# A first half-transfer on ACT's queue, weights loaded later, and convergence products placed in pairs between the last additions

## The chip, the cores and the metric

The kernel runs on one core of one Trainium2 chip. The metric is the device time of one execution in microseconds, taken as the median of three runs. Less is better. A profile was taken of one further execution. Its own time and the span between its first and last instruction stand in the table below.

## The reference, cut to what matters

The input `x` has four images of 128 channels and 64 x 64 = 4096 positions (tokens), all in float32. Three stages follow each other:

```python
# layer 0: attention over channels of a convolution, no causal mask
q, k, v = wq @ x, wk @ x, wv @ x            # 64 x 4096 per image
att = softmax(k.T @ q, over j)              # 4096 x 4096
x   = x + wo @ (att @ v.T).T

# layer 1, attention: on layer-normalised tokens t (4096 x 128)
t = t + softmax(causal(q @ k.T / sqrt(128))) @ v

# layer 1, recurrence: batch-normalised wx_t, 4096 steps per image
y_t = sigmoid(wx_t + y_{t-1} @ V.T)
out = t + y                                  # in the layout of x
```

## The kernel before

The program has two parts. `fast_path` computes everything under two assumptions that it tests on the way: that the softmax denominators stay in a safe range, and that the recurrence forgets its start. The result of the tests is one integer, `flag`. After `fast_path`, every engine loads `flag` (L1277) and branches (L1278); `general_path`, a slow version for the other case, is skipped with these inputs.

**Attention.** The work is a list of items, each a pair of 128-key tiles against one block of 512 queries. `scores` (L894 in layer 0, L903 in layer 1) makes the products on TensorE, ACT takes the exponential (L908, L910), DVE adds up the denominators (L932, L934), and `values` (L954, L962) multiplies by the values two items later. This part lasts from about 14 us to 1975 us.

**The start of image 0.** Layer 0 needs the keys and queries in both halves of the partitions. `cols0` makes the product of 512 columns with `[wq|wk]` (`wqk`, h = 0) and with `[wk|wq]` (`wkq`, h = 1), copies each out of PSUM into `kr` (DVE for h = 0 at L539, ACT for h = 1 at L537), and a DMA (L541) copies 64 partitions of `kr` to the other 64 partitions of `swap`. `vals0` (L547) and `vals0_by_tokens` (L572) make the values. The first scores need the h = 0 half of the first `swap`. The order in the source is: `cols0`, `vals0` of block 0, `cols0` of block 1, `vals0_by_tokens` of block 0, then the items. The list `side` holds the other blocks; one of its tasks goes between two items.

**Queues.** SP's queue issues the eight transfers of `x` of image 0 (L426, 256 KB each) and, behind them, the `swap` transfers. ACT's queue issues the three first weights (`wqk`, `wkq`, `wv0`, L414) in five transfers. POOL's queue issues the weights that come later: `wo2`, `wqT`, `wkT`, `wv1` (L414), and `wf`, `vf`, `gamma`, `beta` (L513). Twelve products of `ident` with itself (L496) run on TensorE before the first real product.

**The recurrence and the end.** Time is cut in 256 chunks of 16 steps per image. All chunks run at once, first ten warm-up steps and then 16 real ones, four images in turn: product (L1156, PE), addition (L1158, DVE), sigmoid (L1161, ACT). For images 0 and 1 POOL adds the residual (L1168) and SP stores (L1170). For images 2 and 3, `residual` transposes the states back (L1184, PE, four at a time into one of four PSUM buffers), DVE adds them to `xr` (L1186, 16 additions in all), and SP stores from `xr` (L1191, 12 stores, 4 MB in all). The test of the recurrence compares each image's state after the last step with its start: two products per image into PSUM (L1203 with `ident`, L1204 with `minus`), and on ACT a sum of squares (L1206). `judge` counts (L1212, L1213, DVE), sums over partitions (L1215, PE), and DVE writes `flag` (L1220). `in_range(True)`, called in `third` of the last block, tests the last four denominators in four DVE instructions (L704 to L707).

The order of the instructions on each engine is decided by a scheduler when the program is built; `keep_in_program_order` binds an instruction to the order of the source.

Of the kernel before, what the change touches and what calls it, by code (L numbers as in the profile page):

```python
# [9 lines left out]
F32 = mybir.dt.float32  # L10
AF = mybir.ActivationFunctionType
ALU = mybir.AluOpType
# [3 lines left out]
P = 128  # L16
BLK = 512
# [3 lines left out]
STEPS = 16  # L21
BY_C = 2
# [337 lines left out]
def fast_path(  # L360
# [22 lines left out]
    nc = tc.nc  # L383
    B, C, N = x.shape
    M = c_wqT.shape[1]
    assert C == P and M == P // 2 and N % CHUNK == 0
    NT = N // P
# [66 lines left out]
    wfc = const.tile([P, P], F32, name="wfc")  # L454
    gamma = const.tile([P, 1], F32, name="gamma")
    beta = const.tile([P, 1], F32, name="beta")
    wo2 = load(nc.gpsimd, "wo2", [P, P], (top, c_woT), (bottom, c_woT))
    wqT = load(nc.gpsimd, "wqT", [P, P], (whole, a_wqT))
    wkT = load(nc.gpsimd, "wkT", [P, P], (whole, a_wkT))
    wv1 = load(nc.gpsimd, "wv1", [P, P], (whole, a_wv))  # L460
    good = const.tile([P, 2], F32, name="good")
    g1 = const.tile([P, P], F32, name="g1")
    recs = const.tile([P, 2, B, NT], F32, name="recs")
# [18 lines left out]
    with tc.tile_pool(name="batch", bufs=1) as batch, tc.tile_pool(name="rows", bufs=2) as rowp, tc.tile_pool(  # L482
# [9 lines left out]


        wp = misc("warm_ps")
        for _ in range(12):
            nc.tensor.matmul(wp[:, :P], lhsT=ident, rhs=ident, start=True, stop=True)  # L496

        def form_half():
# [7 lines left out]
        def form():  # L506
            gp = misc("g_ps")
            nc.tensor.matmul(gp[:, :P], lhsT=wqT, rhs=wkT, start=True, stop=True)
            nc.vector.tensor_copy(g1, gp[:, :P])

        def load_rest():
            for t, src in ((wf, f_wT), (vf, f_vT), (gamma, f_gamma), (beta, f_beta)):
                nc.gpsimd.dma_start(out=t, in_=src)  # L513

        class Batch:
            pass
# [7 lines left out]
        def cols0(b, m):  # L524

            bt = bs[b]
            if m == 0:
                bt.kr = batch.tile([P, 2, N // 2], F32, tag="kr", name="kr")  # L530
                bt.swap = batch.tile([P, N // 2], F32, tag="swap", name="swap")
                bt.v = batch.tile([P, NT // 2, 2, M], F32, tag="v", name="v0")
            for h, w in enumerate((wqk, wkq)):
                ps = misc("kr_ps")
                nc.tensor.matmul(ps, lhsT=w, rhs=xs[:, b, ts(m + h * NB // 2, BLK)], start=True, stop=True)
                if h:
                    nc.scalar.copy(bt.kr[:, h, ts(m, BLK)], ps)  # L537
                else:
                    nc.vector.tensor_copy(bt.kr[:, h, ts(m, BLK)], ps)  # L539
                rows, keys = slice(M - h * M, P - h * M), slice(h * M, h * M + M)  # L540
                nc.sync.dma_start(out=bt.swap[keys, ts(m, BLK)], in_=bt.kr[rows, h, ts(m, BLK)])  # L541

        def vals0(b, m):

# [154 lines left out]
        def in_range(last):  # L699

            r = recs.rearrange("p l b t -> p (l b t)")
            r = r[:, -TPB:] if last else r[:, :-TPB]
            r2 = wk.tile([P, BLK], F32, tag="den", name="r2")[:, : r.shape[-1]]
            nc.vector.tensor_scalar(r2, r, LOW, None, ALU.is_ge)  # L704
            nc.vector.tensor_scalar(r, r, HIGH, None, ALU.is_le)
            nc.vector.tensor_tensor(r, r, r2, ALU.mult)
            nc.vector.tensor_reduce(good[:, 1:2] if last else good[:, 0:1], r, AX.X, ALU.add)  # L707
# [50 lines left out]
        def finish1(b, g):  # L758
# [12 lines left out]
            def first():  # L771
                if final:

                    nc.scalar.activation(spare, agg[:, 0:1], AF.Sigmoid)
                denominators(1, b, g, mem["own"])
                joined(1, b, g, projected(1, agg))
                if final:
                    warm(9, agg[:, : BLK // 2])
                if b >= BY_C:
                    nc.sync.dma_start(  # L780
                        out=x2t[b - BY_C, ts(g, BLK)].rearrange("(j p) c -> p j c", p=P),
                        in_=xs[:, b, ts(g, BLK)].rearrange("p (j c) -> p j c", c=P),
                    )
                mem["xh"] = wk.tile([P, TPB, P], F32, tag="xh2", name="xh2")
                mem["of"] = moments(b, g)

            def norm():
                normed(b, g, mem["xh"], *mem["of"], final)
# [32 lines left out]
            def third():  # L821

                to = xs[:, b, ts(g, BLK)].rearrange("p (s c) -> p s c", s=STEPS)
                if final:
                    in_range(True)
                    for k in range(2):
                        wp = misc("wx_ps")[:, : BLK // 2]
                        nc.tensor.matmul(wp, lhsT=wfc, rhs=mem["xhT"][:, ts(k, BLK // 2)], start=True, stop=True)
                        nc.vector.bn_stats(ends[:, 3 + 6 * k : 9 + 6 * k], wp)
                        nc.scalar.copy(to[:, :, ts(k, CPB // 2)], wp.rearrange("p (c s) -> p s c", s=STEPS))  # L830
                    warm(6, mem["xhT"][:, : BLK // 2])
                    return
                wp = misc("wx_ps")
                nc.tensor.matmul(wp, lhsT=wf, rhs=mem["xhT"], start=True, stop=True)
                nc.vector.bn_stats(stats[:, b * NB + g], wp)  # L835
                if b == B - 1 and g == NB - 2:
                    ahead()
                    in_range(False)
                nc.scalar.copy(  # L839
                    to.rearrange("p s (j q u) -> p s j q u", q=Q, j=TPB),  # L840
                    wp.rearrange("p (q j u s) -> p s j q u", q=Q, j=TPB, s=STEPS),
                )
# [208 lines left out]
        for s in range(len(items) + SKEW + 16):  # L1051
            begin(s)
            if SKEW < s < len(items) - 1 and items[s - SKEW].first and items[s + 1].layer == 0:
                ended = items[s - SKEW - 1]
                if ended.layer == 0 and ended.g not in visits[0]:
                    begin(s + 1)
            if 0 <= s - SKEW < len(items):
                it = items[s - SKEW]
                values(it)
                if it.last:  # L1060
                    rows()
                    tokens()
                    for k, g in enumerate(visits[it.layer].get(it.g, ())):
                        push(s, bs[it.b].leave[g](8 * k))
                    push(s, (finish1 if it.layer else finish0)(it.b, it.g))
            if s < len(items):
                sums(items[s])
            due = [w for w in waiting if w[0] <= s]
            if due:
                w = min(due, key=lambda w: w[0])  # L1070
                waiting.remove(w)
                w[1]()
                push(s, w[2])
            elif side:
                side.pop(0)()
                if not side and items[s].b == 0 and items[s].layer == 0:
                    tokens()
                    load_rest()
                    form_half()
        assert not waiting and not side  # L1080

# [5 lines left out]
    with tc.tile_pool(name="xr", bufs=1) as xrp, tc.tile_pool(name="y", bufs=2) as yp, tc.tile_pool(  # L1087
# [87 lines left out]
            if s >= 0:  # L1175
                add(s)

        def residual(b, pairs=True, then=None):

            for h in range(HALVES):  # L1180
                for s0 in range(0, STEPS, TPB):
                    ps = ps_r.tile([P, TPB, P], F32, tag="r", name="yT_ps")
                    for j in range(TPB):
                        nc.tensor.transpose(ps[:, j], states(b, s0 + j)[:, h], ident)  # L1184
                    t = xr[:, b - BY_C, h, ds(s0, TPB)]
                    tc.keep_in_program_order(nc.vector.tensor_tensor(t, t, ps, ALU.add))  # L1186
                    if pairs and h == 0 and not s0 % (2 * TPB):
                        continue
                    part = slice(s0 - TPB, s0 + TPB) if pairs and h == 0 else slice(s0, s0 + TPB)
                    tc.keep_in_program_order(  # L1190
                        nc.sync.dma_start(out=by_chunk(out_t)[b - BY_C, h, :, part], in_=xr[:, b - BY_C, h, part])  # L1191
                    )
                if then and h == 0:
                    then()

        for b in range(BY_C, B - 1):
            residual(b)


        gap = xrp.tile([P, B], F32, name="gap")  # L1200
        for b in range(B):
            ps = ps_y.tile([P, NCH], F32, tag=f"y{b}", name="gap_ps")
            nc.tensor.matmul((grid if b < BY_C else pair)(ps), lhsT=ident, rhs=prev[b], start=True, stop=False)  # L1203
            nc.tensor.matmul(ps, lhsT=minus, rhs=start[:, b, 1:], start=False, stop=True)  # L1204
            sq = yp.tile([P, NCH], F32, tag=f"y{b}", name="sq")
            nc.scalar.activation(sq, ps, AF.Square, accum_out=gap[:, b : b + 1])  # L1206
        count = xrp.tile([P, B + 2], F32, name="count")
        nc.vector.tensor_copy(count[:, B:], good)

# [5 lines left out]
            nc.tensor.matmul(tp, lhsT=total, rhs=ones, start=True, stop=True)  # L1215
            return tp

        got = []
        residual(B - 1, then=lambda: got.append(judge()))
        nc.vector.tensor_scalar(flag, got[0], P * (B + 2 * B * NT) - 0.5, None, ALU.is_lt)  # L1220


# [62 lines left out]
```

## Time and profile before

| what | value |
|---|---|
| median of three runs | 2053.53 us (2053.29 to 2053.88) |
| the profiled execution's own time | 2054.28 us |
| its span, first to last instruction | 2052.6 us |
| granted TensorE clock, mean | 0.999 |
| PE busy | 2036.8 us (99%) |
| DVE busy | 1486.6 us (72%) |
| ACT busy | 989.1 us (48%) |
| POOL busy | 137.5 us (7%) |
| DMA, mean over the span | 43 GB/s |

The page gives the busy time of each engine, then the span in 40 slices, the DMA queues, the chain of work that ended last and the costliest groups of instructions. A matmul in float32 appears as two records; PE is the matmul, PEld its weight load. In lines of the timeline the columns are: start in us from the span's start, duration or stretch in us, engine, line of the kernel, operation, destination and sources, count, and in brackets the idle time before and what ended it. A letter q behind an engine's name (SPq, ACTq) means its sequencer, which issues DMAs. The time from a DMA's issue to its landing is given beside the issue. Line numbers are those of the kernel before.

### The profile page before, as it was taken

Reading aid. Unit: us, or ns where it says so; the run is one execution under the profiler, and the core shown is the slowest. Engines: PE = TensorE matmul, PEld = TensorE weight load, DVE = VectorE, ACT = ScalarE, POOL = GpSimd, SP = SyncE. Lnnn points to the kernel's source line nnn. Section 1 sums busy time; section 2 is a strip of 40 time slices with the busy share of each in tenths; the row PEclk is TensorE's granted clock in tenths of the full one; section 3 lists DMA queues with packets and bytes.
Section 4 is the critical chain, followed back from the end, with each engine's and each line's share of the span. In section 5 each row is a group of like instructions: output and inputs, shape, how many; then the busy total and the mean of one; then the engine's idle time right before and its main releaser. Section 6 shows DMA issues by size and latency. Waiting matters only on the chain. (4 is left out here: it accounts for less than half of the span.)

```text
span 2052.6 us, 30794 instructions
## 1 busy us (share of the span) xinstructions
PE 2036.8 (99%) x11646; PEld 907.4 (44%) x11646; DVE 1486.6 (72%) x2862; ACT 989.1 (48%) x1071; POOL 137.5 (7%) x237
## 2 busy tenths in 40 slices
PE   9999999999999999999999999999999999999998
PEld 3643354444333345444433335444433334544456
DVE  4799877555889987555588997654578998765568
ACT  4666632323666653333466663333356665333346
POOL 1000011000000011000000001100000000100004
PEclk9999999999999999999999999999999999999999
DMA  3111021231201112222111001123000110210056
GB/s 88 53 33 27 12 42 37 51 79 37 58 2 23 22 22 42 47 62 67 22 53 22 17 17 42 37 68 82 16 17 2 22 23 12 52 42 21 21 115 225
DMA packets 237869, 89.03 MB, mean 43 GB/s; under 512 B 174752, under 2 KB 219296, under 8 KB 237200
## 3 DMA queue, kind: packets, MB, share of 16 engines
q1 hardware_dynamic: 236704, 86.42, 17.7%
q8 instruction: 93, 1.52, 0.3%
q14 instruction: 64, 0.52, 0.1%
q0 software_dynamic: 288, 0.39, 0.1%
q10 hardware_dynamic: 720, 0.16, 0.0%
HBM read 45.84 MB, written 36.89 MB: 40 GB/s over the span
## 5 line engine op out<-in xcount | busy, mean ns | idle before, releaser
L934 DVE TENSOR_TENSOR dsum<-dsum,p 128x1024 f32<-128x1024 f32 x676 | 826.1, 1222 | 429.6 <-ACT p L910 308.5
L908 ACT ACTIVATE p<-s_ps,nshift 128x1024 f32<-128x1024 f32 x512 | 569.3, 1116 | 318.4 <-PE s_ps L894 310.3
L910 ACT ACTIVATE p<-s_ps 128x1024 f32<-128x1024 f32 (+2 forms) x288 | 274.2, 952 | 609.5 <-PE s_ps L903 607.1
L954 PE MATMUL acc<-p,v 64*64 64x512 f32 x4096 | 543.0, 590 | 0.0
L894 PE MATMUL s_ps<-swap,kr 64*64 64x512 f32 x2048 | 539.0, 591 | 2.1 <-DMA swap<-kr 1.2
L894 PE MATMUL s_ps<-kr 64*64 64x512 f32 x2048 | 525.0, 591 | 0.0
L903 PE MATMUL s_ps<-rows,xhT 128*128 128x512 f32 (+3 forms) x1152 | 502.9, 559 | 0.0
L962 PE MATMUL acc<-p,xh 128*128 128x512 f32 (+3 forms) x1152 | 500.9, 557 | 0.0
L962 PEld LDWEIGHTS acc<-p,xh 128*128 128x128 f32 x1152 | 216.2, 190 | 244.3 <-issue 234.2
L903 PEld LDWEIGHTS s_ps<-rows,xhT 128*128 128x128 f32 x1152 | 214.0, 190 | 243.3 <-issue 203.4
L954 PEld LDWEIGHTS acc<-p,v 64*64 64x64 f32 x4096 | 166.6, 133 | 272.5 <-issue 251.6
L894 PEld LDWEIGHTS s_ps<-swap,kr 64*64 64x64 f32 x2048 | 151.4, 133 | 132.3 <-issue 107.7
L894 PEld LDWEIGHTS s_ps<-kr 64*64 64x64 f32 x2048 | 140.7, 133 | 138.0 <-issue 133.6
L666 POOL TENSOR_TENSOR ln_rstd<-ln_var,mhalf 128x4 f32<-128x4 f32 x64 | 68.2, 1065 | 1099.4 <-DVE ln_var L664 1099.4
L942 DVE TENSOR_TENSOR dsum<-dsum,p 128x256 f32<-128x256 f32 (+1 forms) x120 | 55.4, 497 | 64.3 <-POOL p L914 64.3
L652 DVE SCALAR_TENSOR_TENSOR xs<-o_ps,recs,xs 128x128 f32<-128x128 f32 x256 | 74.4, 341 | 3.1
L682 DVE TENSOR_SCALAR xh<-xs,ln_mv,ln_rstd 128x128 f32<-128x128 f32 x252 | 70.2, 342 | 2.2
L914 POOL TENSOR_SCALAR_AFFINE_SELECT p<-p 128x128 f32<-128x128 f32 x128 | 35.9, 304 | 486.4 <-ACT p L910 473.9
L661 DVE BATCH_NORM_STATS2 ln_st<-xs 128x6 f32<-128x128 f32 x256 | 63.2, 269 | 0.0
L932 DVE COPY dsum<-p 128x1024 f32<-128x1024 f32 x60 | 41.0, 683 | 16.0 <-ACT p L910 10.8
L839 ACT COPY xs<-wx_ps 128x512 f32<-128x512 f32 x31 | 18.1, 585 | 65.6 <-DVE stats L835 63.5
L1158 DVE SCALAR_TENSOR_TENSOR z<-xs,scale,y_ps 128x256 f32<-128x256 f32 x100 | 45.0, 480 | 2.6 <-PE y_ps L1156 1.6
(148 smaller groups left out, 989.6 us busy)
## 6 DMA issues: line engine op xcount, KB each, us to landing
xs<-in_xT SPq DMA_DIRECT2D x32, 256.0 KB, 3.0
by_r<-sqT SPq DMA_DIRECT2D x128, 64.0 KB, 2.2
xhT<-by_r SPq DMA_DIRECT2D x128, 64.0 KB, 2.0
by_c<-sqT SPq DMA_DIRECT2D x124, 64.0 KB, 1.8
xhT<-by_c SPq DMA_DIRECT2D x31, 256.0 KB, 2.7
xs<-in_x SPq DMA_DIRECT2D x12, 512.0 KB, 5.9
swap<-kr SPq DMA_DIRECT2D x32, 128.0 KB, 2.3
x2c<-sqT SPq DMA_DIRECT2D x64, 64.0 KB, 2.4
```

What stands on the lines that cost most here:

```text
L652: nc.vector.scalar_tensor_tensor(t, in0=op[:, ts(j, P)], scalar=rec[:, j : j + 1], in1=t, op0=ALU.mult, op1=ALU.add)
L661: nc.vector.bn_stats(st[:, j], xs[:, b, ds(g * BLK + j * P, P)])
L666: nc.gpsimd.tensor_tensor(y, var, mhalf, ALU.pow)
L682: nc.vector.tensor_scalar(dst[:, j], xs[:, b, ds(g * BLK + j * P, P)], mv[:, j, 0:1], y[:, j : j + 1], ALU.subtract, ALU.mult)
L894: nc.tensor.matmul(ps[c * M : c * M + M, off : off + n], lhsT=bs[it.b].kr[part, h, ds(t % (NT // 2) * P + c * M, M)], rhs=rows[h], start=True,
L903: nc.tensor.matmul(ps[:, off : off + n], lhsT=lhsT, rhs=rhs, start=True, stop=True)
L908: nc.scalar.activation(it.p[:, :off], ps[:, :off], AF.Exp, bias=nshift)
L910: nc.scalar.activation(it.p[:, :off], ps[:, :off], AF.Exp, scale=float(P) ** -0.5)
L934: nc.vector.tensor_tensor(flat, flat, it.p, ALU.add)
L942: nc.vector.tensor_tensor(den[:, h, q0:], den[:, h, q0:], it.p[:, o : o + n], ALU.add)
L954: nc.tensor.matmul(bt.acc[h * M : h * M + M, r], lhsT=bt.v[part, t % (NT // 2), t // (NT // 2)], rhs=it.p[part, o : o + n], start=it.first ...
L962: nc.tensor.matmul(bt.acc[:, 0, q0:], lhsT=bt.xh[:, t], rhs=it.p[:, o : o + n], start=it.first and h == 0, stop=it.last and h == 1,)
```

## The change

The change has six edits. (1) The first of the eight `swap` transfers (image 0, block 0, h = 0) is issued from ACT's queue and no more from SP's. (2) The later weights, nine transfers, each wait for a small copy on POOL that reads a column of block 4 of `x`, so that they are issued only once that block has landed; `load_rest` is gone. (3) The warm-up products are seven, not twelve. (4) The four instructions of `in_range(True)` move from `third` to the place after `moments`, the first of them bound to program order. (5) The products of the convergence test, `meet`, now follow each half of `residual`, one image after each half, with the order bound. (6) `judge` and `flag` come after all additions of `residual`, and no more between the halves of the last image.

```diff
-    wo2 = load(nc.gpsimd, "wo2", [P, P], (top, c_woT), (bottom, c_woT))
-    wqT = load(nc.gpsimd, "wqT", [P, P], (whole, a_wqT))
-    wkT = load(nc.gpsimd, "wkT", [P, P], (whole, a_wkT))
-    wv1 = load(nc.gpsimd, "wv1", [P, P], (whole, a_wv))
+    wo2 = const.tile([P, P], F32, name="wo2")
...
+    late = ((wqT, a_wqT), (wkT, a_wkT), (wo2[0:M], c_woT), (wo2[M:P], c_woT), (wv1, a_wv))
+    late += ((wf, f_wT), (vf, f_vT), (gamma, f_gamma), (beta, f_beta))
+    for t, src in late:
+        nc.gpsimd.tensor_copy(t[:, 0:1], xs[: t.shape[0], 0, (NB // 2) * BLK : (NB // 2) * BLK + 1])
+        nc.gpsimd.dma_start(out=t, in_=src)
...
-        for _ in range(12):
+        for _ in range(7):
             nc.tensor.matmul(wp[:, :P], lhsT=ident, rhs=ident, start=True, stop=True)
...
-        def load_rest():
-            for t, src in ((wf, f_wT), (vf, f_vT), (gamma, f_gamma), (beta, f_beta)):
-                nc.gpsimd.dma_start(out=t, in_=src)
...
-                nc.sync.dma_start(out=bt.swap[keys, ts(m, BLK)], in_=bt.kr[rows, h, ts(m, BLK)])
+                queue = nc.sync if b or m or h else nc.scalar
+                queue.dma_start(out=bt.swap[keys, ts(m, BLK)], in_=bt.kr[rows, h, ts(m, BLK)])
...
-            nc.vector.tensor_scalar(r2, r, LOW, None, ALU.is_ge)
+            ins = nc.vector.tensor_scalar(r2, r, LOW, None, ALU.is_ge)
+            if last:
+                tc.keep_in_program_order(ins)
...
                 mem["of"] = moments(b, g)
+                if final:
+                    in_range(True)
...
                 if final:
-                    in_range(True)
...
-                    load_rest()
                     form_half()
...
-        def residual(b, pairs=True, then=None):
+        def residual(b, pairs=True):
...
-                        nc.tensor.transpose(ps[:, j], states(b, s0 + j)[:, h], ident)
+                        ins = nc.tensor.transpose(ps[:, j], states(b, s0 + j)[:, h], ident)
+                        if not j and s0 + TPB == STEPS:
+                            pin(ins)
...
-                if then and h == 0:
-                    then()
-        for b in range(BY_C, B - 1):
-            residual(b)
+                meet((b - BY_C) * HALVES + h)
...
-        for b in range(B):
+        pin = tc.keep_in_program_order
+        def meet(b):
             ps = ps_y.tile([P, NCH], F32, tag=f"y{b}", name="gap_ps")
-            nc.tensor.matmul((grid if b < BY_C else pair)(ps), lhsT=ident, rhs=prev[b], start=True, stop=False)
+            shaped = grid if b < BY_C else pair
+            pin(nc.tensor.matmul(shaped(ps), lhsT=ident, rhs=prev[b], start=True, stop=False))
             nc.tensor.matmul(ps, lhsT=minus, rhs=start[:, b, 1:], start=False, stop=True)
...
-        got = []
-        residual(B - 1, then=lambda: got.append(judge()))
-        nc.vector.tensor_scalar(flag, got[0], P * (B + 2 * B * NT) - 0.5, None, ALU.is_lt)
+        for b in range(BY_C, B):
+            residual(b)
+        tp = judge()
+        nc.vector.tensor_scalar(flag, tp, P * (B + 2 * B * NT) - 0.5, None, ALU.is_lt)
```

The built program of the changed kernel differs from that of the kernel before only at the two ends. At the start, on PE, one of the two products of scores with `swap` moves ahead of the second block's key products, and on ACT the `swap` transfer stands before the load of the activation table. Around the last block, a few DVE instructions change places. At the end, PE's order is: remaining transposes of a half, two products of `meet`, and so four times, then the product of `judge`. Between, each engine's order is the same.

More of the change, by code (lines that the diff above doesn't have):

```diff
@@ L456, in fast_path @@
     beta = const.tile([P, 1], F32, name="beta")
-    wo2 = load(nc.gpsimd, "wo2", [P, P], (top, c_woT), (bottom, c_woT))
-    wqT = load(nc.gpsimd, "wqT", [P, P], (whole, a_wqT))
-    wkT = load(nc.gpsimd, "wkT", [P, P], (whole, a_wkT))
-    wv1 = load(nc.gpsimd, "wv1", [P, P], (whole, a_wv))
+    wo2 = const.tile([P, P], F32, name="wo2")
+    wqT = const.tile([P, P], F32, name="wqT")
+    wkT = const.tile([P, P], F32, name="wkT")
+    wv1 = const.tile([P, P], F32, name="wv1")
+    late = ((wqT, a_wqT), (wkT, a_wkT), (wo2[0:M], c_woT), (wo2[M:P], c_woT), (wv1, a_wv))
[3 more added lines that the diff above has]
+        nc.gpsimd.dma_start(out=t, in_=src)
     good = const.tile([P, 2], F32, name="good")
@@ L1216, in judge @@
             return tp
-        got = []
-        residual(B - 1, then=lambda: got.append(judge()))
-        nc.vector.tensor_scalar(flag, got[0], P * (B + 2 * B * NT) - 0.5, None, ALU.is_lt)
+        assert HALVES * (B - BY_C) == B
+        for b in range(BY_C, B):
+            residual(b)
+        tp = judge()
+        nc.vector.tensor_scalar(flag, tp, P * (B + 2 * B * NT) - 0.5, None, ALU.is_lt)
 def kernel(
```

## The prediction

> **What bounds the kernel now.** I read the page first, then the waits of the first 20 us, the timelines of both ends, and the DMA queues at the end.
>
> ```profile
> span 2052.6 us, 30794 instructions
> PE 2036.8 (99%) x11646; PEld 907.4 (44%) x11646; DVE 1486.6 (72%) x2862; ACT 989.1 (48%) x1071; POOL 137.5 (7%) x237
> ```
>
> PE is the bound: only 15.8 us of the span are without a matmul. The built program is the same from about 14 to 1975 us, so only the ends can move, and all that is worth anything there is when the first scores start and when the last engine arrives.
>
> The start, from the waits and the timeline:
>
> ```profile
> PE s_ps L894 <- DMA swap<-kr: 1.2, 1, 1.2
> ...
> 2.61 5.03 PE L496 MATMUL warm_ps<-ident 128*128 128x128 f32 x24 [2.61 <-POOL ident masks.py:199]
> ...
> 7.47 1.02 PE L535 MATMUL kr_ps<-xs,wqk 128*128 128x512 f32 x2
> ...
> 8.53 0.69 DVE L539 COPY kr<-kr_ps 128x512 f32<-128x512 f32 x1 [4.28 <-PE kr_ps L535]
> 9.25 4.13 SPq L541 DMA_DIRECT2D swap<-kr  x4
> ...
> 10.29 1.12 PE L535 MATMUL kr_ps<-xs,wqk 128*128 128x512 f32 x2
> ...
> 12.20 0.66 PE L572 MATMUL vT_ps<-ident,vT 128*128 128x128 f32 x4
> ...
> 14.05 0.65 PE L894 MATMUL s_ps<-swap,kr 64*64 64x512 f32 x2 [1.19 <-DMA swap<-kr]
> ```
>
> The warm-up occupies PE until 7.6, although `wqk` landed at 1.25 + 4.3 = 5.55 and the first block of `x` at 0.82 + 3.8 = 4.6. The first `swap`, issued at 9.25, lands 4.8 later at 14.05, behind the transfers of `x` on the same queue; PE idles 1.2 for it. From 14 on PE is full (5.95 of 6.00 us busy between 14 and 20).
>
> The end, from the timeline, the branch line, the windows and the queues:
>
> ```profile
> 2040.25 2.48 DVE L1186 TENSOR_TENSOR xr<-xr,yT_ps 128x512 f32<-128x512 f32 x4 [1.40 <-PE yT_ps L1184]
> 2042.65 0.16 DVE L1212 TENSOR_SCALAR count<-gap 128x4 f32<-128x4 f32 x1
> ...
> 2043.38 0.15 DVE L1220 TENSOR_SCALAR flag<-tp 1x1 int32<-1x1 f32 x1 [0.38 <-PE tp L1215]
> 2043.46 2.46 DVE L1186 TENSOR_TENSOR xr<-xr,yT_ps 128x512 f32<-128x512 f32 x4
> ...
> L1278 PEldq COMPARE_BRANCH  x1: 4635/4635/4635, 2044.8 to 2044.8; - x1
> ...
> 2036.50:2045.50 9.00, 7.21 (x53) 6.14 (x51) 7.19 (x15) 1.43 (x6) 0.00 (x0) 1.00 1.01 393
> ```
>
> The additions end at 2045.92, but the 16 DMA engines are full (share 1.01, 393 GB/s) from 2036.5 on: the stores set the end, not DVE. The store issued at 2044.15 lands in 2.1 us; the last three, issued at 2044.75, 2045.35 and 2045.94, need 4.8, 4.9 and 4.9. From 2048.6 to 2050.4 the store queue holds 6.2% of 16 engines, which is one engine alone. Between 2045.8 and 2048.0 four packets of the instruction queues (q14, q8) were served. So one engine fell behind by about 2.5 us, while code was fetched for the branch. The last landing is at 2050.8, and 1.8 us of semaphore resets and barriers follow.
>
> **What the Trainium skill says.** "TensorE: Matmul & The Clock Gate", section "What's actually happening": the clock is at half until about 3.4 us of activity, and falls after an idle window of that length. The trace agrees: warm-up records are 0.21 us apart until 6.6 us, then 0.11; at the end the granted clock falls near 2048.3, some 4.6 us after the last matmul. "DMA: Bandwidth & Descriptors", "Queues, rings and completion order": each DMA engine takes turns between the queues, so a transfer on another queue passes the backlog but shares the engines. The 4.8 against 2.2 us for later `swap` transfers on empty engines agrees with the first half; nothing before shows the second for `swap`. "Runtime: NRT & Kernel Launch", "Instruction fetch mechanics": a taken branch whose target isn't loaded forces a fetch by DMA. The 4.63 us of PE's branch and the q8 and q14 packets agree. "ScalarE: Activation LUTs", "What ACT_TABLE_LOAD costs": about 1.28 us; the trace has 1.28.
>
> **The change, part by part, in the profiled execution's time.**
>
> Warm-up: 24 records become 14. At 0.213 apart, the first key product may start at 2.98 + 13 x 0.213 = 5.75, not 7.47; its inputs are there at 5.55. But the clock is still at half until about 6.8, so its two passes take 0.85 and about 0.55 and not 0.43 each. The second starts at 6.6, done for DVE about 7.35 (before: 7.90 + 0.63 = 8.53). DVE's copy ends at 8.05 (before 9.22): 1.2 gained so far.
>
> `swap` on ACT: issued at 8.05. Its landing time is not in the trace. Bounds: 2.2 us (empty engines) and 4.0 (five transfers on ACT's queue beside `x` took 3.9 to 5.0 early on). I take 2.8, as the engines are still busy with `x` but the backlog is passed: 10.85. Queued behind it on ACT, because ACT stands waiting for DVE, are the table load (1.28, hidden at 3.19 before) and the h = 1 copy: 8.05 + 0.46 + 1.28 = 9.8, ending 10.4 (before 9.97). PE needs that copy's PSUM buffer for the second block's key products. SP's queue loses one issue; its second `swap` waits for the 10.4 copy but serves query block 4 only, many items later: nothing.
>
> PE's order: one scores product with `swap` now stands ahead of the second block's key products, so PE waits for 10.85 first, and these, their copies and the value transposes wait behind it. It takes two passes, 0.95 with the mode switch (estimate from passes 0.43 to 0.5 apart). Key products of block 1 start at 11.8, later than ACT's 10.4, which is thus covered. From there the row before gives 12.20 - 10.29 = 1.91 to the transposes and 0.59 (17.09 to 17.68) to scores: 14.3, against 14.05. **Start: +0.25**, from -0.35 (landing 2.2) to +1.45 (4.0). So the 1.2 gained is eaten by the order of PE.
>
> Weights later: nine POOL copies at 0.19 (L1028, longest 1.12) and nine issues at 0.55, from about 5.4: issued by 12, at worst by 20; landing takes up to 6.7. First use is at 37.8 (L508): **0**. If that cover were gone, PE would wait the difference. The traffic of 0.39 MB moves from 3.5-11 to about 8-16, where it shares with `swap`; the 4.0 bound takes it in.
>
> `in_range`: the four instructions of 0.14 to 0.17 move out of places where DVE waits for PE (L704) or overlaps (L705 to L707) into POOL's 1.01 us of `ln_rstd` or between dependent steps 0.2 apart. **0**, within 0.1 either way.
>
> Meeting products and count: the work is equal (4 x 0.87 us of products). Before, images 2 and 3 stood together and DVE idled 1.40 before the ninth addition; count to flag took another 0.81 of DVE. Both leave the additions: the ninth starts about 2038.8 and the last ends at 2045.92 - 2.2 = 2043.7. By itself this is nothing, as the DMA engines were full: from the sixth store's landing (2040.0 + 3.0) the last 2.1 MB need 5.3 us at 393 GB/s, 2048.3. The flag becomes later: last products 2043.2, ACT 0.38 + 0.19, then count to flag 0.88 as before: 2044.9 against 2043.53. The loads (1.06 to 1.12) and the branches move to 2046.2, and the fetch, which came 1.1 after the branch, to 2047.3, when about 0.5 us of stores is left per engine. Two ends: the fetch stalls its engine 2.2 as before, landing 2047.3 + 2.2 + 0.5 + 0.5 = 2050.5 and the end at 2052.3; or stores are through, and the last to come is PE's branch, which costs 2.7 (ACT's, from 2044.7 to 2047.5) to 4.63: 2048.9 to 2050.8, plus about 1.2 to 1.8 of resets. I take 2051.7, **-0.9** (from -1.7 to +0.3).
>
> **Sum:** +0.25 + 0 + 0 - 0.9 = -0.65. Span 2052.6 becomes 2051.95; the profiled execution's own time was 2054.28, that is 0.75 over the median. On the median: 2053.53 - 0.65 = 2052.9.
>
> **Rivals.** About 0.2% (4.1 us) is what can be told from no change here.
> (a) Forecast, 50%: 2052.9.
> (b) `swap` lands in 2.2 and stores finish ahead of the fetch: -0.35 - 1.7 gives 2051.5. For it: fewer transfers early. Against: 87% of the engines' time went to SP's queue between 7.5 and 11.5. 20%.
> (c) The branch becomes the bound at its full 4.63, and the start costs 0.9: +0.9 + 0.1 gives 2054.5. For it: PE's fetch comes after those of ACT and DVE. 25%.
> (d) Slower: PE now idles from about 9.1 to 10.85 after a shorter warm-up, and the clock falls back. Each 3.4 us window at half speed costs 1.7; two with the waiting give +0.25 + 3.4 - 0.9: 2056.3. It decides from an idle of one window, 3.4 us, which a landing of `swap` after 12.5 would bring; three windows without the tail's gain pass 0.2%. Against: 1.2 us of idle before 14.05 did no harm. 5%.
> That the change doesn't do what it says is excluded by the built order, except that the early transfer is paid back on PE, which (a) counts.
>
> **Range.** (a)'s own spread is 2051.9 to 2053.9; with (b) and most of (c): 2051.2 to 2054.7. Faster than 0.2% 0.01, slower 0.03, same 0.96.
>
> **What would show it.** First key product near 5.75; `swap` landing near 10.9; scores of the first item complete near 15.3 (14.3 plus about 1.1); the table load after `swap`'s issue; no 1.40 idle in the additions, last one ending near 2043.7; flag near 2044.9; last store landing before 2050.5. I am wrong if `swap` lands outside 10.3 to 12, if PE's second block goes ahead of the scores, or if the end hangs on neither the stores nor the branch.

## The result and the profile after

The changed kernel takes 2060.16 us (median of 7 runs, 2058.79 to 2062.0), the kernel before 2053.35 in the same comparison (7 runs, 2053.1 to 2053.88). The ratio is 1.0034, with a 95% interval from 1.0024 to 1.0044: it is slower by 6.8 us, and the forecast was 2052.9. The profiled execution took 2061.27 with a span of 2059.6, which is 7.0 more than the span before.

All of it was lost in the first 22 us. Lines of the timeline (columns as in the section on the profile):

```profile
1.57 3.36 PE L502 MATMUL warm_ps<-ident 128*128 128x128 f32 x14 [1.57 <-POOL ident masks.py:199]
...
5.95 2.04 PE L537 MATMUL kr_ps<-xs,wqk 128*128 128x512 f32 x2 [1.02 <-DMA wqk<-in_c_wkT]
...
8.03 0.69 DVE L541 COPY kr<-kr_ps 128x512 f32<-128x512 f32 x1 [4.81 <-PE kr_ps L537]
...
14.81 1.97 PE L902 MATMUL s_ps<-swap,kr 64*64 64x512 f32 x2 [3.73 <-DMA swap<-kr]
...
16.71 2.07 PE L537 MATMUL kr_ps<-xs,wqk 128*128 128x512 f32 x2
...
20.28 0.80 PE L576 MATMUL vT_ps<-ident,vT 128*128 128x128 f32 x4
...
22.02 1.08 PE L551 MATMUL v_ps<-xs,wv 128*64 128x512 f32 x4
```

The last line is the value product of block 1. It started at 15.07 before and starts at 22.02 now, 6.95 later. The first addition of the end (L1195) starts at 2040.95 and started at 2033.99 before, 6.96 later. So nothing was lost or gained between, and from that addition on the end takes 18.6 in both.

Three things are to be seen. TensorE stands 3.73 us for `swap`, where it stood 1.19. The scores pass, the key products and the transposes of block 1 now come behind that wait. And they run at half speed: a pair of key passes takes 2.07, where the same pair took 1.12. The windows of 2 us of TensorE (the window and its length, TensorE's busy time with the number of matmuls, the granted clock, the DMA share and GB/s) show when:

```profile
10.00:12.00 2.00, 1.08 (x4) 1.00 1.05 300
12.00:14.00 2.00, 0.00 (x0) 0.96 0.70 139
14.00:16.00 2.00, 1.19 (x2) 0.50 0.08 19
16.00:18.00 2.00, 2.00 (x3) 0.50 0.00 0
18.00:20.00 2.00, 2.00 (x3) 0.50 0.00 0
20.00:22.00 2.00, 2.00 (x11) 0.83 0.29 66
```

Finer windows place the fall and the rise:

```profile
13.50:14.00 0.50, 0.00 (x0) 0.84 0.35 70
...
20.40:20.80 0.40, 0.40 (x4) 0.67 0.27 72
```

A mean of 0.84 over the half microsecond to 14.0 is a fall from 1 to 0.5 at 13.84; a mean of 0.67 from 20.4 to 20.8 is a rise at 20.66. The clock was at half for 6.82 us. The column can be read only from its first change on: in the kernel before it shows 1.00 from 2 to 7 us too, while the warm-up records stand 0.21 us apart, twice as far as after 7.0.

Now the transfer. From the timeline, four of the issues:

```profile
7.00 0.74 POOL L466 DMA_DIRECT2D wqT<-in_a_wqT  x1
7.74 0.56 POOL L466 DMA_DIRECT2D wkT<-in_a_wkT  x1
...
8.76 0.52 ACTq L545 DMA_DIRECT2D swap<-kr  x1
9.30 0.59 POOL L466 DMA_DIRECT2D wv<-in_a_wv  x1
```

And the DMA view of the same 24 us (KB each, median us from issue to landing):

```profile
swap<-kr ACTq DMA_DIRECT2D x1, 128.0 KB, 6.0
wqT<-in_a_wqT POOLq DMA_DIRECT2D x1, 64.0 KB, 6.6
wkT<-in_a_wkT POOLq DMA_DIRECT2D x1, 64.0 KB, 6.2
...
wv<-in_a_wv POOLq DMA_DIRECT2D x1, 64.0 KB, 5.7
```

Issue plus latency gives landings at 13.6, 13.9, 14.8 and 15.0, and at 13.3 for the last load of `x` (SP's queue, issued at 6.79, 6.5 us): in the order of issue, across three queues. (Among all transfers of this start, a pair issued close together lands out of order by 0.24 us at most.) `swap` on ACT's queue did not pass what stood on the others. It needs 6.0 us, longer than the 4.8 on SP's queue before.

At the end, the view of the stores' line L1200, whose longest latency is that of the last store, and the branch:

```profile
L1200 SPq DMA_DIRECT2D out_x<-xr x12: 345/616/1151, 2042.9 to 2052.2; - x12
...
DMA to landing us min/median/max: 3.0/3.7/5.5
```

```profile
L1289 PEldq COMPARE_BRANCH  x1: 5512/5512/5512, 2052.7 to 2052.7; - x1
```

The additions end at 2050.60 (0.68 after the start of the last at 2049.91), in the old time scale (6.96 off) at 2043.64. But the last store, issued at 2052.24, still lands late, 5.5 us on, and TensorE's branch takes 5.51 where it took 4.63. The span ends at 2059.6, which is 2052.64 in the old scale: the end gained nothing.

### The profile page after: what moved, and what is told of

Its sections match the earlier page's. It is cut to its first block, busy times and chain, and to the rows that moved or that the text cites. A ratio compares the mean times of both kernels' runs of the same rounds, so it can differ in the third digit from the quotient of the medians.

```text
span 2059.6 us, 30786 instructions
## 1 busy us (share of the span) xinstructions
PE 2040.9 (99%) x11636; PEld 907.5 (44%) x11636; DVE 1486.9 (72%) x2862; ACT 989.8 (48%) x1071; POOL 137.1 (7%) x246
## 4 chain that ended last, share of the span: by engine, by line
PE 98%; DMA 1%; DVE 0%; ACT 0%; issue 0%; SPq 0%; ACTq 0%; POOL 0%
PE s_ps L911 22%; PE acc L970 22%; PE s_ps L902 22%; PE acc L962 21%; PE o_ps L646 3%; PE y_ps L1163 2%; PE kr_ps L537 1%; PE r_ps L599 1%; PE wx_ps L842 1%; PE v_ps L551 1%; DMA xc<-x2c 0%; PE yT_ps L1191 0%; DMA swap<-kr 0%; DMA wqk<-in_c_wkT 0%; ACT p L916 0%
```

## The experiments

The theory: one edit, `swap` on ACT's queue, lets the scheduler put a scores product ahead of block 1's key products; TensorE then stands for a transfer that is not faster, the clock falls, and the block behind it runs slowly. The rivals are the shorter warm-up, the transfer itself, and the weights held back. Each kernel was run several times against the kernel before on the same chip, whose medians lie between 2053.3 and 2053.5; different variants ran on different chips. The intervals are about 0.002 wide, which is 4 us: differences of one or two microseconds between variants are only firm where the traces show them too, and a trace is one execution of each.

**Order put back (e_order).** The changed kernel, with these products bound to the order of the source:

```diff
-                nc.tensor.matmul(ps, lhsT=w, rhs=xs[:, b, ts(m + h * NB // 2, BLK)], start=True, stop=True)
+                ins = nc.tensor.matmul(ps, lhsT=w, rhs=xs[:, b, ts(m + h * NB // 2, BLK)], start=True, stop=True)
+                if not b and m < 2:
+                    tc.keep_in_program_order(ins)
...
+                        if it is items[0] and not h and not c:
+                            tc.keep_in_program_order(ins)
```

> The changed kernel, with the key products of block 1 kept ahead of the first scores product on TensorE. Theory (order and clock): the loss of 6.8 us is 0.8 of later landing, 1.9 of a scores pass taken alone and 4.3 of key products and transposes that stand behind it, 2.7 of these because the clock fell while TensorE waited; with the order back, TensorE works through the wait, the scores start at the landing near 14.8, and the time is 2053.9 to 2055.0. Rival (the transfer on ACT's queue and the late weights themselves): the order changes little, 2058 or more.

Measured: 2054.49, ratio 1.0006 (0.9998 to 1.0015). 5.7 of the 6.8 are gone. The timeline of TensorE:

```profile
10.05 1.13 PE L537 MATMUL kr_ps<-xs,wqk 128*128 128x512 f32 x2 [1.28 <-ACT kr L541]
...
14.26 0.65 PE L904 MATMUL s_ps<-swap,kr 64*64 64x512 f32 x2 [1.64 <-DMA swap<-kr]
...
15.28 1.08 PE L553 MATMUL v_ps<-xs,wv 128*64 128x512 f32 x4
```

Here `swap` is issued at 7.57 and lands at 14.21 (6.6 us later): no better. But the key products fill the wait at full speed, the clock does not fall in the 1.64 us that are left of it, and the value product of block 1 starts at 15.28. The wait for ACT (1.28) is the one of the copy behind the table load; with the landing at 14.21 it costs nothing.

**Twelve warm-up products again (e_w12).** The changed kernel with

```diff
-        for _ in range(7):
+        for _ in range(12):
```

> The changed kernel with 12 warm-up products again. Theory (order and clock): key products start near 6.5 at full clock and the copy ends near 8.0, but the transfer still lands near 14, TensorE still stands 4 us before it, and block 1 still waits behind it: 2056.5 to 2059.5. Rival (the shorter warm-up alone is the cause): 2053.0 to 2054.5.

Measured: 2060.0, ratio 1.0035 (1.0021 to 1.0048); a little over the theory's upper end, far from the rival. In the profile TensorE is done with block 0 at 8.74, stands 4.8 us, and the scores pass after it still takes 1.97. So the shorter warm-up is not the cause of the 6.8.

**`swap` back on SP's queue (e_sp).** The changed kernel with

```diff
-                queue = nc.sync if b or m or h else nc.scalar
+                queue = nc.sync
```

> The changed kernel with the first transfer of the halves on SP's queue again; by the built order this also puts block 1's key products back ahead of the first scores and the table load back ahead of the transfer. Theory (order and clock): 2053.2 to 2054.8, scores near 14.0 to 15.3, as the short warm-up and the later weights cost little by themselves. Rival (short warm-up, clock at half through the head): 2056 or more. Rival (later weights slow the transfer): landing after 15, 2054.5 to 2056.

Measured: 2054.54, ratio 1.0008 (1.0000 to 1.0017). This undoes the queue, and by the scheduler's decision the order of TensorE and of the table load as well; it ends where `e_order` ends, which undoes only TensorE's order. So the queue by itself is worth nothing measurable. `swap`, issued at 8.43, lands at 14.19, as it does from ACT's queue; the rival of the later weights had named a landing after 15.

**The end alone (e_tail).** The kernel before, with edits 4 to 6 of the change and no other; their core:

```diff
-                if then and h == 0:
-                    then()
+                meet((b - BY_C) * HALVES + h)
...
-        residual(B - 1, then=lambda: got.append(judge()))
+        for b in range(BY_C, B):
+            residual(b)
+        tp = judge()
```

> The kernel before with only the two edits of the end (meeting products in pairs with the count behind all additions, and the range test moved). Theory (the end gains nothing, since a code fetch holds up one DMA engine's stores wherever the branch stands): 2053.1 to 2053.8. Rival (the gain of 0.9 of the prediction is there, but hidden in the changed kernel): 2052.3 to 2053.0.

Measured: 2053.72, ratio 1.0002 (0.9994 to 1.0011). There is no gain of 0.9. From the first addition (2033.03) to the end of the span (2051.6) it takes 18.57, the kernel before 18.61.

**One edit alone (b_act).** The kernel before with

```diff
-                nc.sync.dma_start(out=bt.swap[keys, ts(m, BLK)], in_=bt.kr[rows, h, ts(m, BLK)])
+                queue = nc.sync if b or m or h else nc.scalar
+                queue.dma_start(out=bt.swap[keys, ts(m, BLK)], in_=bt.kr[rows, h, ts(m, BLK)])
```

> The kernel before with one edit: the first transfer of the halves goes out on ACT's queue. By the built order this alone puts one scores product ahead of block 1's key products, and the table load behind the transfer. Theory (order and clock): the transfer lands near 13.3 to 14.2, TensorE stands before it for some 4 us, and a scores pass of 0.95 to 1.9 and key products and transposes of 2.6 to 4.3 come behind it: 2057.0 to 2059.8. Rival (the loss needs the short warm-up or the late weights as well): below 2055.

Measured: 2058.0 (2055.72 to 2059.98), ratio 1.0022 (1.0013 to 1.0031): 4.7 of the 6.8 from this one edit. The time is in the theory's range, but the wait is half of what it said. TensorE's timeline and windows:

```profile
12.95 1.07 PE L895 MATMUL s_ps<-swap,kr 64*64 64x512 f32 x2 [2.06 <-DMA swap<-kr]
13.95 1.14 PE L535 MATMUL kr_ps<-xs,wqk 128*128 128x512 f32 x2
14.91 1.88 PE L535 MATMUL kr_ps<-xs,wkq 128*128 128x512 f32 x2
```

```profile
14.00:15.00 1.00, 1.00 (x4) 0.97 0.04 10
15.00:16.00 1.00, 1.00 (x3) 0.50 0.00 0
...
18.00:19.00 1.00, 1.00 (x8) 0.83 0.41 94
```

The clock falls at 14.94 (0.97 is a fall 0.06 before 15.0), when TensorE has been working again for 2 us, and rises at 18.34, which is 3.4 later. A wait of 2.06 came before it, where the 1.64 of `e_order` did no harm. The DMA view of the last load of `x` (issued at 6.64) and of `swap` (issued at 9.78):

```profile
xs<-in_x SPq DMA_DIRECT2D x1, 256.0 KB, 5.9
...
swap<-kr ACTq DMA_DIRECT2D x1, 128.0 KB, 3.1
```

On the same queue `swap` took 3.1 here and 6.0 in the changed kernel. It was issued later, no held-back weights stood ahead of it, and it landed at 12.9, 0.4 behind the last load of `x` at 12.5.

**The wait filled (e_fill).** The changed kernel in its own order, with idle products (their results are overwritten) before the early scores product, and that order bound. The core of the edit:

```diff
+        ps0 = ps_s.tile([P, 2 * BLK], F32, tag="s", name="s_ps")
+        for _ in range(17):
+            pinned(nc.tensor.matmul(ps0[:, BLK : BLK + P], lhsT=ident, rhs=ident, start=True, stop=True))
+        pinned(nc.tensor.matmul(ps0[0:M, :BLK], lhsT=bs[0].kr[0:M, 0, 0:M], rhs=bs[0].swap[0:M, :BLK], start=True, stop=True))
```

> The changed kernel, in its own order, with 17 extra 128-wide products (34 passes, 3.6 us at full clock; their results are overwritten) on TensorE in the wait for the first transfer. Theory: the clock is then full behind the wait; the pass alone costs 0.95 and the block behind it 2.6 instead of 1.9 and 4.3, so 2.7 of the 6.8 is regained: 2057.0 to 2058.0. Rival (the clock plays no part, the time is the waiting alone): 2060 as before.

Measured: 2058.4 (2057.1 to 2059.07), ratio 1.0024 (1.0015 to 1.0033), 1.8 less than the changed kernel, and 0.4 above the theory's range. The timeline:

```profile
8.38 4.06 PE L1024 MATMUL s_ps<-ident 128*128 128x128 f32 x34
13.43 1.07 PE L1025 MATMUL s_ps<-swap,kr 64*64 64x512 f32 x2 [0.99 <-DMA swap<-kr]
14.43 1.13 PE L539 MATMUL kr_ps<-xs,wqk 128*128 128x512 f32 x2
...
17.93 1.08 PE L555 MATMUL v_ps<-xs,wv 128*64 128x512 f32 x4
```

From the first scores product to the value product it takes 17.93 - 13.43 = 4.50; in the changed kernel 22.02 - 14.81 = 7.21, in the kernel before 15.07 - 14.05 = 1.02. So the 6.95 us that block 1 is late in the changed kernel's profile are 0.76 of later landing (14.81 for 14.05), 3.48 of products that stand behind the wait, at full clock, and 2.71 of the clock, the 2.7 that was expected. The profiled execution is the fastest of the eleven. That the median regains only 1.8 fits with executions in which the clock was not up when the filling began, which no trace here shows.

**Weights not held back (e_order_early, e_early).** The first is `e_order`, the second the changed kernel itself, both with edit 2 undone:

```diff
-        nc.gpsimd.tensor_copy(t[:, 0:1], xs[: t.shape[0], 0, (NB // 2) * BLK : (NB // 2) * BLK + 1])
-        nc.gpsimd.dma_start(out=t, in_=src)
+    wo2 = load(nc.gpsimd, "wo2", [P, P], (top, c_woT), (bottom, c_woT))
+    wqT = load(nc.gpsimd, "wqT", [P, P], (whole, a_wqT))
+    wkT = load(nc.gpsimd, "wkT", [P, P], (whole, a_wkT))
+    wv1 = load(nc.gpsimd, "wv1", [P, P], (whole, a_wv))
...
+                    load_rest()
```

> The kernel with block 1's key products kept ahead (2054.49), and its weights not held back. Theory (transfers land in the order of issue whichever queue they are on, so held-back weights stand ahead of the first transfer of the halves, and leave the engines idle near 5.5 us): the transfer lands 0.5 to 1.0 earlier, 2053.4 to 2054.0. Rival (weights on POOL's queue cost nothing): 2054.5.

> The changed kernel with its weights not held back; queue, order, 7 warm-up products and the edits of the end stay. Theory (the 2.1 between 2058.0 of the one-edit kernel and 2060.16 are the held-back weights: the transfer lands later behind them, and TensorE stands long enough for the clock to fall in most executions): 2057.6 to 2058.8. Rival (the short warm-up or the end makes up the 2.1): 2059.8 to 2060.4.

Measured: 2053.95, ratio 1.0002 (0.9994 to 1.0011), 0.5 below `e_order`; and 2058.89, ratio 1.0027 (1.0016 to 1.0038), 1.3 below the changed kernel and just over the theory's upper end. In their profiles `swap` lands at 13.07 and 12.39, against 14.21 and 14.77 with the weights held back. Part of that is not the weights, as the loads of `x` land earlier there too. What the weights do is seen from the last load of `x` to the landing of `swap`: 0.2 to 0.5 us in the seven profiles in which only `x` and early weights stand ahead of it (kernel before, `e_tail`, `b_act`, `e_early`, `e_order_early` and the two without a branch, below), and 0.9 to 1.5 in the five with the weights held back (changed kernel, `e_order`, `e_w12`, `e_sp` and `e_fill`). Both groups have `swap` on SP's queue and on ACT's. So holding back weights whose first use is at 37.8 delayed a transfer on another queue by about a microsecond; the 0.5 and 1.3 of the medians fit, though their intervals overlap.

**Less ahead of the transfer (b_xlate).** The kernel before, with half of the loads of `x` behind `swap` on SP's queue:

```diff
+    def first_x(ms):
+        for m in ms:
+            for g in (m, m + NB // 2):
+                tc.keep_in_program_order(nc.sync.dma_start(out=xs[:, 0, ts(g, BLK)], in_=x[0, :, ts(g, BLK)]))
...
+                if not (b or m or h):
+                    tc.keep_in_program_order(ins)
+                    first_x(range(2, NB // 2))
```

> The kernel before, with the last four of the eight loads of x (blocks 2, 6, 3 and 7, first used at 19.5) issued behind the first transfer of the halves on SP's queue. Theory (landing in the order of issue): 1 MB less stands ahead of it, so it lands near 11.5 to 12.0 instead of 13.0 to 14.0, scores start at 12.2 right behind the transposes, and the time is 2051.8 to 2052.9. Rival (a transfer takes 4.5 to 6 us here in any case): 2053.4; or the loads held back come too late for block 2: 2054 or more.

Measured: 2052.96, ratio 0.9998 (0.9990 to 1.0006): between the theory's range and the first rival, not to be told from no change. The DMA view of 6 to 12.5 us:

```profile
xs<-in_x SPq DMA_DIRECT2D x4, 256.0 KB, 4.2
swap<-kr SPq DMA_DIRECT2D x1, 128.0 KB, 2.3
```

The transfer lands in 2.3 us on SP's own queue once nothing large is ahead of it. In this execution the warm-up ran at half clock to its end, so key products started at 7.89, the issue was at 9.96, and TensorE was never idle from then on; it had become the limit itself.

**All of it (b_best).** `b_xlate`, with ten warm-up products, and the weights of POOL's queue made to wait for `ident`, which brings `ident` and with it the warm-up forward:

```diff
-        for _ in range(12):
+        for _ in range(10):
...
+    for t, src in late:
+        nc.gpsimd.tensor_copy(t[:, 0:1], ident[: t.shape[0], 0:1])
+        nc.gpsimd.dma_start(out=t, in_=src)
```

> The kernel before, with the last four loads of x behind the first transfer of the halves on SP's queue, the weights of POOL's queue issued behind the identity matrix (which brings the warm-up forward by 1.0), and 10 warm-up products. Theory: key products start near 5.8, the transfer lands 2.3 to 3.0 after an issue near 7.5 to 8.5, TensorE never waits longer than a few tenths, scores start between 11.2 and 12.9: 2051.2 to 2052.6. Rival (with the clock still at half at the key products, the earlier start gives nothing over the 2052.96 of the variant with the loads held back): 2052.7 to 2053.3.

Measured: 2051.59 (2050.79 to 2052.46), ratio 0.9991 (0.9983 to 0.9999), 1.8 faster than the kernel before, by an interval that just leaves out 1, and within the theory's range. Here `swap` is issued at 7.61 and lands 3.0 us later. What each of the three parts gives was not tried. The timeline:

```profile
5.83 1.02 PE L539 MATMUL kr_ps<-xs,wqk 128*128 128x512 f32 x2
...
10.56 0.66 PE L579 MATMUL vT_ps<-ident,vT 128*128 128x128 f32 x4
11.15 0.65 PE L901 MATMUL s_ps<-swap,kr 64*64 64x512 f32 x2
```

**No branch (b_nobranch, t_nobranch).** The kernel before, and `e_tail`, without the last lines; so these two kernels leave out the test of `flag` and the general path:

```diff
-            bad = nc.values_load(flag[0:1, 0:1])
-            with tc.If(bad > 0):
-                general_path(tc, *layer0, *[ins[n] for n in ("in_a_wq", "in_a_wk", "in_a_wv")], *ffn, *y)
```

> The kernel before without the last step: the flag is computed, but it is not loaded, no engine branches on it, and the general path behind the branch is left out. Theory (the fetch of code holds up one DMA engine and with it the last three stores): the last store lands some 2.5 earlier, 2050.5 to 2051.3. Rival (the stores are slow at the end for their own traffic): 2052.8 or more.

> The kernel before with only the two edits of the end, and without the branch and the general path behind it. Theory (the 4 MB of stores at the full DMA rate set the end, in whichever order the additions and the count stand): the same as the other kernel without a branch, within 0.4. Rival (the edits gain 0.9 where no branch hides it): 0.7 to 1.1 below that kernel.

Measured: 2050.34, ratio 0.9984 (0.9977 to 0.9991), 0.2 below the theory's range, and 2050.28, ratio 0.9985 (0.9979 to 0.9992). The DMA view of the first kernel from 2044 to 2046:

```profile
out_x<-xr SPq DMA_DIRECT2D x3, 256.0 KB, 2.4
```

The stores that take 4.8 to 4.9 beside the branch take 2.4 without it, and the two kernels end within 0.1 of each other. The edits of the end gain nothing with the branch and nothing without it. Test, branch and general path together cost 3.05 us of the median. In the profiles, the last store lands 16.8 us after the first addition with them (2033.99 to 2050.8) and 14.35 without (2033.35 to 2047.7): the stores set the end in both, and about 2.5 of the cost is theirs. That a fetch of code holds them up is argued: in the kernel before, the instruction queues q14 and q8 move packets from 2045.8 on, and in these two kernels they move none at the end, but the fetch was not separated from the rest that is left out.

## Why the prediction was wrong

The steps in their order, the profiled execution against the text:

- **Warm-up.** First key product at 5.95 (5.75 forecast): near, but by luck. The forecast had the warm-up start when it did before and fill the time to 5.75. It starts at 1.57 and not at 2.61, because POOL builds `ident` at 1.22 and not at 2.25, behind the issue of `wo`, and it ends at 4.93; TensorE stands 1.02, and the landing of `wqk` starts the key product. The clock was to rise at 6.8, about as before (7.0). It did not: both key products run at half, 2.04 and 1.91 where they took 1.02. DVE's copy ends at 8.72 and not 8.05: 0.7 lost. The experiments do not see this as a cause of its own (`e_w12`).
- **Landing of `swap`.** This is the step that failed most: 2.8 forecast, 6.0 measured, 3.2 lost, and the landing at 14.8 lies outside the 10.3 to 12 that the text set as its own sign of being wrong. The assumption was that the transfer passes the backlog. The upper bound of 4.0 was already below what the text quoted beside it (3.9 to 5.0 for transfers on ACT's queue). And the profile of before had a warning in its DMA view of the issues from 6 to 9.6 us:

```profile
gamma<-in_f_gamma POOLq DMA_DIRECT2D x1, 0.5 KB, 6.1
beta<-in_f_beta POOLq DMA_DIRECT2D x1, 0.5 KB, 6.7
```

  Half a kilobyte on POOL's queue needed over 6 us, behind weights of at most 64 KB on its own queue, while `x` stood on SP's. The text used the 6.7 for the late weights and not for `swap`. It took the 4.8 against 2.2 us of `swap` as agreement with the page; but all those transfers were on SP's queue, and say nothing of another one. The Trainium skill, "DMA: Bandwidth & Descriptors", section "Queues, rings and completion order", says that an engine takes turns between its queues; here landings follow the order of issue whichever queue they are on, and the measurement decides.
- **The scores pass that TensorE takes first.** The mechanism, that block 1's key products wait behind it, was in the text and was right. Its size was not: the pass took 1.9 (0.95 forecast), and from the key products to the next scores it took 4.3 (2.5 forecast). Both were priced at full clock. Together 2.7 lost, about what `e_fill` puts on the clock (2.71).
- The four terms give 0.7 + 3.2 + 0.95 + 1.8 = 6.65, and the forecast of 14.3 for the rest of the first scores became 21.0: the miss of the start is accounted for.
- **Weights later.** Taken as 0, with the remark that the 4.0 covers their sharing. Wrong: about 1 us of the 3.2 above (`e_early`, `e_order_early`).
- **The end.** The additions end at 2043.64 in the old scale (2043.7 forecast) and the flag is there at 2044.76 (2044.9 forecast, though its terms sum to 2044.65): right. The gain of 0.9 was a value between two ends. One, a fetch that again holds up the stores, was given as 2052.3 and is what came (2052.64). In the other the stores escape the code fetch. They don't: the last store is issued at 2045.28 in the old scale, 0.66 earlier than before, and lands 5.5 later. The instruction queues' packets begin at 2047.2 in the old scale, where they began at 2045.8: they have moved with the branch.

Rival (d), with 5%, had the mechanism and the sign. It was dismissed because 1.2 us of idle had done no harm and because it was thought to need an idle of 3.4. The runs show a fall with a wait of 2.06 us (`b_act`), and 2.75 us into the wait of 3.73 in the changed kernel (11.09 to 13.84). Its price of 3.4 for the clock was close (2.7); what it lacked was the late landing, and that pass and block stand behind it.

What stays open: 2058.0 of the single edit and 1.3 for the weights make 2059.3, 0.9 short of 2060.16, which is less than the intervals resolve. Neither the warm-up (-0.2) nor the end (+0.3) was seen outside its interval, and they were not tried together. Nor was it tried what makes the landings follow the order of issue, or how long a wait, at what place, makes the clock fall.

## What to carry to other kernels

Before a transfer is moved to another queue, look in the trace when the transfers issued before it land, whichever queue they are on, and how long small ones on other queues take at that time. Where landings follow the order of issue, as here, only less traffic ahead helps: on SP's queue 4.8 us became 2.3 when 1 MB went behind the transfer. A new queue also moves the scheduler's choices on engines that the edit doesn't name: compare the built order, and bind it where a matmul would stand before a DMA. Price every product that comes behind a wait of TensorE twice, at full and at half clock.

## What the runs showed of the hardware

- The Trainium skill, "TensorE: Matmul & The Clock Gate", section "What's actually happening", speaks of free-running windows of 3.4 us. The trace agrees: the fall at 13.84 and the rise at 20.66 are 6.82 apart, two windows, and in `b_act` fall and rise are 3.4 apart. The page has the clock fall after an idle window. Here it fell earlier: 2.75 us after the last product in the changed kernel, 2.0 in `e_early` (10.12 to 12.12), and in `b_act` at the end of a window (11.53 to 14.94, if windows are 3.41 long) in which TensorE stood only 1.42 us and then worked, with a 64-row scores pass first. Whether the small pass counts for less was not tried.
- Landings of the start followed the order of issue across the queues of SP, ACT and POOL, to within 0.24 us in the changed kernel's trace and 0.8 at most in the others; where no weights were held back, `swap` landed 0.2 to 0.5 us behind the last load of `x` from SP's queue and from ACT's alike.
- The test and branch at the end cost 3.05 us, though `general_path` is only skipped: beside it, the last 256 KB stores took 4.8 to 5.5 us and not 2.4, and TensorE's branch itself 4.6 to 5.5.
